# RWKV filler work on one Trainium2 core: one stream with a single share per unit, mixes between chains

## The chip, the cores and the metric

The kernel runs on one core of a Trainium2 chip. It is one program of four transformer layers in float32. The metric is the device time of one execution in microseconds. Before the change, three runs took 3275.48, 3282.33 and 3282.14 us, a median of 3282.14 us.

The core's engines are named as the profile names them: PE (matmul; PEld is its weight load), DVE (vector), ACT (scalar and activation functions), POOL (GpSimd) and SP (used here for its DMA queue). Each engine runs its own instructions in order and waits on semaphores for others. Some DMAs are issued from SP's queue and some from ACT's.

## The reference

There are 16 sequences of 100 tokens with 512 channels, and a context of 361 tokens for each. Layers 0 and 2 are cross attention (layer 2 with an MLP). Layers 1 and 3 are RWKV blocks, and only they are touched here. A block, cut to what matters (`_ln` is a layer norm with weights):

```python
xa = _ln(x, ln1_w, ln1_b)
sx = concat([state[:, 1:2] - xa[:, :1], xa[:, :-1] - xa[:, 1:]])       # difference of neighbouring tokens
xxx = tanh((xa + sx * maa_x) @ maa_w1).reshape(b, l, 5, 32)
xxx = einsum('blfd,fde->blfe', xxx, maa_w2)
xm = xa[:, :, None] + sx[:, :, None] * (maa_stack + xxx)               # five mixed inputs: k, w, v, r, g
xk, xw, xv, xr, xg = (xm[:, :, j] for j in range(5))
w = exp(-exp(time_decay + tanh(xw @ td_w1) @ td_w2))
r, k, v = xr @ Wr.T, xk @ Wk.T, xv @ Wv.T
g = silu(xg @ Wg.T)
# for each token, 32 heads of 16 channels, state s of 16 x 16 a head:
#   a = k_t v_t^T ; out_t = r_t (u * a + s) ; s = a + w_t * s
og = group_norm(out, gn_w, gn_b)
x1 = x + og * g @ Wo.T
xc = _ln(x1, ln2_w, ln2_b)                                             # channel mixing
sx2 = concat([state[:, 0:1] - xc[:, :1], xc[:, :-1] - xc[:, 1:]])
rr = sigmoid((xc + sx2 * ffn_maa_r) @ Wfr.T)
kk = square(relu((xc + sx2 * ffn_maa_k) @ Wfk.T))
x_out = x1 + rr * (kk @ Wfv.T)
```

## The kernel before

**Tiles.** The 16 sequences are four groups (`NG = 4`, `G = 4` sequences each), so a group's rows are `T = 400` tokens. Channels are four chunks of 128 (`NC = 4`). Activations lie as channels by tokens, 128 x 400, while a layer norm is computed on rows of tokens (100 x 512) and turned by PE transposes.

**The scan and its units.** The recurrence is computed by DVE scans along time. Chunk `C` of 16 (four per group) holds 128 channels of 400 tokens, and it is worked off in 8 units; a layer has `UNITS = 128`. One unit does two of the 16 value columns of each head. On PE, `spread` (two matmuls with `sel` into `vb`) spreads v over the head's rows, one unit ahead. Then come ACT's small copy of the start state into `vb`, DVE's `product` (`vb<-vb,kc`, v times k), two DVE scans (`a<-wc,vb`), POOL's `a<-a,rc` (times r) and, every second unit, PE's `gather` of two units into `acc`. A finished chunk passes through `norm` (the group norm: copies on ACT, the matmul with `mean`, Ln and Exp on ACT, products on POOL). `enter`, `bonus` and `gates` load a chunk's k, w, r, v and g from DRAM scratch on SP's queue and add the `u` term.

**The filler.** Everything else in the layer is cut into `pieces`, each with an estimated PE time in us, a first unit (`slot`) in which it may run, a function and a tag. Each turn of the loop over `u` emits the unit's own work and then takes pieces from the front of the list, skipping those whose slot has not come, until a share `due` of estimated time is used up. Pieces of time 0 are taken as soon as their slot comes. A chain (four matmuls that add up in one PSUM bank) is two pieces that follow each other directly. Instructions are pinned to this order on each engine, while DMAs are placed by a scheduler.

- `projections(g, base)` makes group g's k, v, r, w and g from x. First come the layer norm's `stats` (DVE), `root` (POOL) and `normed` (ACT). Then come `turned` (16 transposes in four pieces), `inner` (the chain with `w1`), `mix` (32-row matmuls with `maa_w2`, then DVE and POOL build the mixed input `xj`), `decay_in` and `decay`, `plain` (the chains with `Wk`, `Wv`, `Wr`) and the gates' chains with `Wg`. The `Wg` chains are kept in `held` and placed in the next group's list. Results are stored to DRAM scratch on ACT's queue; the scratch pool holds two groups.
- `channels(g, slot)` is the channel mixing. It has stats, `normed`, `turned`, keys (chains with `Wfk`), then `gates_of` (`Wfr`) and `values` (`Wfv`) for rows 0 to 3 by turns; rows 3 are a small product.
- `output(g, slot)` is the product with `Wo` and the residual, tag `("wo", g)`, placed at the front of the list when group g's units are done. Later work needs some of these done, and `through(tag)` forces them.

**The order around the change.** Projections of group 0 come before unit 0. Those of group g + 1 are appended at the unit 10 before group g ends (u = 22, 54 and so on). The channel mixing of groups 0 to 2 is appended in one go at u = 118 - 32 = 86, with the stats and transposes of a group placed inside the list of the group before it; that of group 3 at u = 128. In a group's list all mixes of a pair stand together, as do the decays. The share is 2.6 for the first 23 units, then 2.85, 3.7 in the last 32 units and 3.9 after them. Odd units and units 2 and 7 of a chunk get less, since they have work of their own.

Single-buffered tiles (`ext`, `sx`, `z0`, `tz`) and the rings `xm` (4), `tm` (4) and `stage` (6) limit how far groups may overlap, and three PSUM banks `mm` serve all pieces.

Of the kernel before, what the change touches and what calls it, by code (L numbers as in the profile page):

```python
# [17 lines left out]
NC = E // 128  # L18
G = 4
NG = B // G  # L20
# [16 lines left out]
def xattn_sequence(ctx: ExitStack, tc: tile.TileContext, d: dict, out: bass.AP):  # L37
# [196 lines left out]
    some = scratch.enter_context(tc.tile_pool(name="scratch", bufs=1))  # L234
# [462 lines left out]
    def rwkv(n, ws, small, first, next_weights, last):  # L697
# [6 lines left out]
        with ExitStack() as es:  # L704
# [3 lines left out]
                tc.tile_pool(name=f"l{n}a_dram", bufs=2, space=bass.MemoryType.DRAM)  # L708
# [26 lines left out]
            put = {}  # L735
# [133 lines left out]
            def projections(g, base):  # L869
# [59 lines left out]
                behind = [(p[0], base - 1 if g > 1 or i > 3 else -1000, *p[2:]) for i, p in enumerate(held)]  # L929
# [134 lines left out]
                for i in range(G):  # L1064
                    piece(0.0, lambda i=i: normed(i), base)
                for c in range(NC):
                    piece(0.45, lambda c=c: turned(c), base + 1)
                late = base + 2

                def mix(fs, c):  # L1070
                    piece(1.0 if len(fs) > 1 else 0.9, lambda: mixed(fs, c), late)

                pieces.extend(behind[:2])
                inner()
                pieces.extend(behind[2:6])
# [12 lines left out]
                for c in range(NC):  # L1088
                    plain(3, "Wr", "r", c)
                for c in range(NC):  # L1090
                    mix((4,), c)
                held[:] = written(lambda: [gate(co) for co in range(NC)])

            def channels(g, slot):


# [64 lines left out]
                def values(i):  # L1161
# [22 lines left out]
                some = lambda fn, n: written(lambda: [piece(0.01, lambda i=i: fn(i), slot) for i in range(n)])  # L1184
                root, normed = ln_apply(st, [xb[g * G + i] for i in range(G)], xn, nm)
                return {
                    "stats": some(stats, G) + written(lambda: piece(0.01, root, slot)),
                    "normed": some(normed, G),
                    "turned": written(lambda: [piece(0.45, lambda c=c: turned(c), slot) for c in range(NC)]),
                    "first": written(lambda: [keys(co) for co in range(NC)] + [gates_of(0), values(0)]),  # L1190
                    "second": written(lambda: [gates_of(1), values(1), gates_of(2), values(2)]),
                    "third": written(lambda: gates_of(3)),
                    "fourth": written(lambda: values(3)),
                }

            def channel_stream(groups, slot):

                got = []
                parts = [channels(g, slot) for g in groups]
                for k in ("stats", "normed", "turned"):  # L1200
                    got += parts[0][k]
                got += [(p[0], slot - 1, *p[2:]) for p in held]
                held.clear()
                for p, q in zip(parts, parts[1:] + [{"stats": [], "normed": [], "turned": []}]):
                    got += p["first"] + q["stats"] + p["second"] + q["normed"]
                    got += p["third"] + q["turned"] + p["fourth"]
                return got


# [138 lines left out]
            UNITS = 32 * NG  # L1348
            u, due = -42, 0.0
            while u < UNITS + 6 or pieces or slots.due or slots.late:  # L1350
# [3 lines left out]
                g = (u + 10) // 32  # L1354
                if u % 32 == 22 and g + 1 < NG:
                    projections(g + 1, u + 7)
                elif u % 32 == 22 and g + 1 == NG:
                    pieces.extend(channel_stream(range(NG - 1), u + 7))
                elif u % 32 == 0 and u > 0:
                    if u == UNITS:  # L1360

                        kept = max(len(pieces) - 4, 0)
                        for i in range(kept, len(pieces)):
                            pieces[i] = (pieces[i][0], u + 8, *pieces[i][2:])
                        own = channel_stream([NG - 1], u + 8)
                        pieces[kept:kept] = own[: G + 1]
                        pieces.extend(own[G + 1 :])
# [30 lines left out]
                due = min(due, 0.0) + (2.6 if 0 <= u < 23 else 2.85 if u < UNITS - 32 else 3.7 if u < UNITS else 3.9)  # L1398
# [369 lines left out]
    def load(layer, *names):  # L1768
        return {k: load_w(d[f"L{layer}_{k}"], f"l{layer}_{k}") for k in names}
# [80 lines left out]
```

## Time and profile before

One execution was profiled. Its own time is 3275.75 us; the span that the trace covers is 3274.0 us. Layers 1 and 3 have the same plan. The stretches below are cut at the first and last DVE product `vb<-vb,kc` of each layer; idle is the length less PE's busy time, and PEclk is the mean granted clock of PE as a share of full speed.

| stretch (us from the span's start) | length | PE busy | PE idle | DVE busy | POOL busy | PEclk |
|---|---|---|---|---|---|---|
| layer 1 before unit 0 (663.9 to 765.7) | 101.8 | 85.1 | 16.7 | 30.4 | 37.0 | 0.81 |
| layer 1, starts of units 0 to 127 (765.7 to 1356.6) | 590.9 | 527.6 | 63.3 | 444.9 | 400.3 | 0.89 |
| layer 1 after that (1356.6 to 1454.3) | 97.7 | 74.2 | 23.5 | 22.8 | 18.9 | 0.87 |
| layer 3 before unit 0 (2499.0 to 2598.9) | 99.9 | 85.1 | 14.8 | 28.9 | 33.5 | 0.80 |
| layer 3, starts of units 0 to 127 (2598.9 to 3182.7) | 583.8 | 521.3 | 62.5 | 444.8 | 400.2 | 0.90 |
| layer 3 after that (3182.7 to 3274.0) | 91.3 | 74.2 | 17.1 | 18.9 | 16.7 | 0.90 |

Mean durations of the instructions that recur, from the page's groups and the timeline: DVE product 982 ns, scan 973 ns (two a unit), the DVE part of a mix (`tm`) 624 ns, POOL's `a` product 1885 ns, the POOL part of a mix (`xj`) 961 ns. A PE matmul in float32 shows as two records of the same shape, while `spread` shows as one.

How to read it: an engine's busy time does not say that it sets the pace. PE is the busiest, but a busy PE may be running at half clock, and what ends its idle stretches is another engine's work. The stretches of a few units tell more than the whole loop, since the filler is not the same from one to the next.

### The profile page before, as it was taken

The numbers are of one execution on the slowest core, as the hardware profiler recorded it, in microseconds if no ns is written. First come the engines' busy times: TensorE is split into PE (matmuls) and PEld (weight loads), VectorE is DVE, ScalarE is ACT, GpSimd is POOL, SyncE is SP. The second block draws the span as 40 slices with busy tenths as digits, with TensorE's granted clock in tenths as the row PEclk, the third lists the DMA queues.
The fourth block names the chain that finished last, engine by engine and source line by source line (L and its number), as shares of the span: only waits on it lengthen the run. The fifth ranks groups of instructions, "written<-read, shape, count | busy, mean of one in ns | idle before, by whom it ended". The sixth has DMA issues, their size and how long they took to land. (4 is left out here: it accounts for less than half of the span.)

```text
span 3274.0 us, 44343 instructions
## 1 busy us (share of the span) xinstructions
PE 2970.2 (91%) x16403; PEld 1523.1 (47%) x16403; DVE 1647.3 (50%) x3309; ACT 1235.9 (38%) x2883; POOL 1161.1 (35%) x1058
## 2 busy tenths in 40 slices
PE   7999898888898989879999999899998998898997
PEld 4555555534344444334555555445554443444443
DVE  2555555625877777523433333321001388877761
ACT  4777677722423343322232323211111233334332
POOL 0111111135677675422212111210001467676651
PEclk9999999978889899989999999999998888999998
DMA  6101010022222432130000010020011322324211
GB/s 195 33 23 33 23 41 18 1 88 71 91 84 89 131 102 86 47 101 20 20 21 20 21 33 19 27 70 11 7 52 30 108 96 69 104 83 135 89 32 51
DMA packets 134690, 193.98 MB, mean 59 GB/s; under 512 B 19806, under 2 KB 102686, under 8 KB 134474
## 3 DMA queue, kind: packets, MB, share of 16 engines
q1 hardware_dynamic: 102218, 145.26, 14.8%
q10 hardware_dynamic: 32256, 45.89, 3.8%
q8 instruction: 129, 2.11, 0.3%
q14 instruction: 87, 0.71, 0.1%
HBM read 115.20 MB, written 49.15 MB: 50 GB/s over the span
## 5 line engine op out<-in xcount | busy, mean ns | idle before, releaser
L88 POOL TENSOR_TENSOR a<-a,rc 128x800 f32<-128x800 f32 x256 | 481.6, 1885 | 245.7 <-DVE a L88 194.5
L88 DVE TENSOR_TENSOR_SCAN a<-wc,vb 128x400 f32<-128x400 f32 x512 | 477.3, 973 | 42.3 <-PE acc L93 20.8
L88 DVE CUSTOM_DVE_ANT_0 pr<-l_sc,mask 100x361 f32<-100x361 f32 x512 | 252.0, 528 | 144.8 <-PE l_sc L93 144.7
L88 DVE TENSOR_TENSOR vb<-vb,kc 128x792 f32<-128x792 f32 x256 | 251.5, 982 | 136.6 <-ACT vb L88 135.4
L88 ACT ACTIVATE pr<-pr,nm 100x361 f32<-100x361 f32 x512 | 301.3, 593 | 4.6 <-POOL sums L88 3.7
L96 PEld LDWEIGHTS l_pT<-ident,pr 100*121 100x121 f32 x1536 | 193.2, 186 | 103.8 <-issue 50.4
L93 PE MATMUL vb<-xc,sel 128*128 128x400 f32 x512 | 217.9, 509 | 12.4 <-DVE a L88 12.2
L1542 DVE CUSTOM_DVE_ANT_0 junk<-l2a_sc,mask 100x361 f32<-100x361 f32 x256 | 136.9, 535 | 182.3 <-PE l2a_sc L93 165.1
L96 PE MATMUL l_pT<-ident,pr 100*121 100x100 f32 x1536 | 216.3, 276 | 6.3 <-ACT pt L88 4.3
L1578 POOL TENSOR_TENSOR pa<-pt,pt 121x1600 f32<-121x1600 f32 x16 | 57.1, 3571 | 364.1 <-ACT pt L1573 364.1
L88 ACT COPY vb<-s 128x8 f32<-128x8 f32 x256 | 44.3, 173 | 365.4 <-PE vb L93 329.8
L88 ACT COPY pt<-l_pT 121x400 f32<-121x400 f32 x256 | 125.1, 489 | 146.5 <-PE l_pT L96 145.6
L88 POOL TENSOR_TENSOR xj<-tm,ext 128x400 f32<-128x400 f32 x160 | 149.5, 961 | 82.9 <-DVE tm L88 82.9
L93 PE MATMUL v<-l_v_w,ct 128*121 128x512 f32 x384 | 177.2, 605 | 0.0
L1763 DVE TENSOR_TENSOR x<-pb,x 100x512 f32<-100x512 f32 x16 | 12.9, 804 | 320.0 <-DMA pb<-po 311.1
L74 PE MATMUL h<-yTb,l_fc 128*128 128x400 f32 x512 | 172.8, 500 | 0.6 <-ACT yTb L339 0.6
L93 PE MATMUL k<-ct,l_k_w 128*128 128x361 f32 x512 | 170.7, 476 | 0.0
L74 PE MATMUL p<-l_proj,h 128*128 128x512 f32 x384 | 165.5, 592 | 0.0
L93 PEld LDWEIGHTS vb<-xc,sel 128*128 128x128 f32 x512 | 99.5, 208 | 131.8 <-issue 80.9
L88 POOL TENSOR_SCALAR ve<-mv 100x1 f32<-100x1 f32 x16 | 3.6, 223 | 406.8 <-DVE mv L88 406.8
L88 DVE SCALAR_TENSOR_TENSOR tm<-mm,vec,sx 128x400 f32<-128x400 f32 x160 | 94.6, 624 | 102.5 <-PE mm L93 90.9
L93 PE MATMUL l_sc<-kz,qz 32*100 32x361 f32 x1024 | 112.2, 508 | 34.3 <-DVE nm L88 32.1
(282 smaller groups left out, 5194.2 us busy)
## 6 DMA issues: line engine op xcount, KB each, us to landing
ct<-in_ctxT SPq DMA_DIRECT2D x32, 722.0 KB
dk<-k ACTq DMA_DIRECT2D x32, 200.0 KB
kc<-dk SPq DMA_DIRECT2D x32, 200.0 KB
dw<-wd ACTq DMA_DIRECT2D x32, 200.0 KB
wc<-dw SPq DMA_DIRECT2D x32, 200.0 KB
dv<-v ACTq DMA_DIRECT2D x32, 200.0 KB
dhi<-hi ACTq DMA_DIRECT2D x32, 200.0 KB
dlo<-lo ACTq DMA_DIRECT2D x32, 200.0 KB
```

The lines of the kernel that those rows point to most:

```text
L74: nc.tensor.matmul(out=ps, lhsT=lhs(c), rhs=rhs(c), start=(c == 0), stop=(c == n - 1))
L88: return lambda *args, **kw: tc.keep_in_program_order(op(*args, **kw))
L93: pin(nc.tensor.matmul(**kw))
L96: pin(nc.tensor.transpose(out, in_, ident))
L1542: nc.vector.tensor_tensor_reduce(out=junk, in0=ss[r][:L, :S2], in1=t["mask"], scale=-1.0, scalar=FLT_MAX, op0=ALU.add, op1=ALU.min, accum_ ...
L1578: nc.gpsimd.tensor_tensor(t["pa"], t["pt"][0], pt, ALU.add)
L1763: nc.vector.tensor_tensor(x, pb[:, i, :], x, ALU.add)
```

## The change

The change is in the function `rwkv` alone. The diff, cut to its core:

```diff
-                tc.tile_pool(name=f"l{n}a_dram", bufs=2, space=bass.MemoryType.DRAM)
+                tc.tile_pool(name=f"l{n}a_dram", bufs=3, space=bass.MemoryType.DRAM)
...
-                behind = [(p[0], base - 1 if g > 1 or i > 3 else -1000, *p[2:]) for i, p in enumerate(held)]
+                behind = list(held)
...
-                    piece(0.0, lambda i=i: normed(i), base)
+                    piece(0.0, lambda i=i: normed(i), base - 1 + i // 2)
                 for c in range(NC):
-                    piece(0.45, lambda c=c: turned(c), base + 1)
-                late = base + 2
+                    piece(0.45, lambda c=c: turned(c), base + 1 + c if g else base + 1)
+                late = base + (5 if g else 2)
...
-                pieces.extend(behind[:2])
+                pieces.extend(behind[:4])
                 inner()
-                pieces.extend(behind[2:6])
                 for c in range(NC):
                     mix((0, 1), c)
+                    pieces.extend(behind[4 + 2 * c : 6 + 2 * c])
                 decay_in()
-                pieces.extend(behind[6:])
                 for c in range(NC):
                     plain(0, "Wk", "k", c)
-                for c in range(NC):
                     mix((2, 3), c)
-                for co in range(NC):
-                    piece(0.9, lambda co=co: decay(co), late)
                 for c in range(NC):
                     plain(2, "Wv", "v", c)
+                    piece(0.9, lambda c=c: decay(c), late)
                 for c in range(NC):
                     plain(3, "Wr", "r", c)
-                for c in range(NC):
                     mix((4,), c)
...
-            def channels(g, slot):
+            def channels(g, base, pace):
+                slot = base + (3 if pace else 1)
...
+                    "stats": written(
+                        lambda: [piece(0.0, lambda i=i: stats(i), base - 6 + i) for i in range(G)]
+                        + [piece(0.0, root, base - 2)]
+                        + [piece(0.0, lambda i=i: normed(i), base - 1 + i // 2) for i in range(G)]
+                    ),
+                    "turned": written(lambda: [
+                        piece(0.45, lambda c=c: turned(c), base + 1 + (c // 2 if pace else 0)) for c in range(NC)
+                    ]),
+                    "rest": written(
+                        lambda: [keys(co) for co in range(NC)]
+                        + [fn(i) for i in range(4) for fn in (gates_of, values)]
+                    ),
...
-            def channel_stream(groups, slot):
...
+            def channel_stream(g, slot, pace=True):
+                part = channels(g, slot, pace)
+                pieces.extend(part["stats"])
+                pieces.extend(held)
                 held.clear()
...
+                pieces.extend(part["turned"] + part["rest"])
...
-            UNITS = 32 * NG
-            u, due = -42, 0.0
+            UNITS, LEAD = 32 * NG, (24.0, 30.0)
+            u, due, blended = -42, 0.0, 0
...
-                if u % 32 == 22 and g + 1 < NG:
-                    projections(g + 1, u + 7)
-                elif u % 32 == 22 and g + 1 == NG:
-                    pieces.extend(channel_stream(range(NG - 1), u + 7))
...
-                    output(g - 1, u + 7)
-                if u == UNITS - 32 - 3:
-                    cm.update(load(n, "Wfk", "Wfr", "Wfv"))
+                if u == UNITS:
+                    for i in range(max(len(pieces) - 8, 0), len(pieces)):
+                        pieces[i] = (pieces[i][0], u + 9, *pieces[i][2:])
+                if u % 32 == 0 and 0 < u <= UNITS:
+                    output(u // 32 - 1, u + 7)
+                short = sum(p[0] for p in pieces) < LEAD[len(put) == NG]
+                if u == -42:
+                    projections(0, u + 7)
+                elif short and u > -16 and len(put) < NG:
+                    projections(len(put), u + 8)
+                elif short and len(put) == NG and blended < NG:
+                    g = blended
+                    if u >= 32 * g + 40 and not any(p[3] == ("wo", g) for p in pieces):
+                        if g == 0:
+                            cm.update(load(n, "Wfk", "Wfr", "Wfv"))
+                        channel_stream(g, u + (8, 8, 4, 2)[g], g < NG - 1)
+                        blended += 1
...
-                due = min(due, 0.0) + (2.6 if 0 <= u < 23 else 2.85 if u < UNITS - 32 else 3.7 if u < UNITS else 3.9)
+                due = min(due, 0.0) + (2.9 if 0 <= u < UNITS else 3.9)
```

In words: projections and channel mixing are appended when the estimated time of the pieces left falls below 24 us (30 us once all projections are in the list), in the order of the groups, instead of at fixed units. The share is 2.9 in every unit of the loop. Mixes and decays stand between chains one at a time. The stats, the normalised rows and the transposes of a group get slots a unit or half a unit apart. The channel mixing of groups 1 to 3 is no longer woven into the one before. The weights of the channel mixing are asked for when its first group is appended, and the DRAM scratch holds three groups.

More of the change, by code (lines that the diff above doesn't have):

```diff
@@ L1182, in values @@
                     )
-                some = lambda fn, n: written(lambda: [piece(0.01, lambda i=i: fn(i), slot) for i in range(n)])
                 root, normed = ln_apply(st, [xb[g * G + i] for i in range(G)], xn, nm)
                 return {
[L1187 to L1193, printed above, removed]
-                }
@@ L1196, in channel_stream @@
-            def channel_stream(groups, slot):
[L1198 to L1202, printed above, removed]
+                    "stats": written(
[3 more added lines that the diff above has]
+                    ),
@@ L1203, in channel_stream @@
                 held.clear()
[L1204 to L1207, printed above, removed]
+                pieces.extend(part["turned"] + part["rest"])
             chunks = {}
@@ L1353, in rwkv @@
                     nws[""] = first_stats(f"a{n}", vector, gpsimd)
-                g = (u + 10) // 32
-                if u % 32 == 22 and g + 1 < NG:
-                    projections(g + 1, u + 7)
-                elif u % 32 == 22 and g + 1 == NG:
-                    pieces.extend(channel_stream(range(NG - 1), u + 7))
[L1359 to L1367, printed above, removed]
-                    output(g - 1, u + 7)
-                if u == UNITS - 32 - 3:
-                    cm.update(load(n, "Wfk", "Wfr", "Wfv"))
+                if u == UNITS:
[15 more added lines that the diff above has]
+                        blended += 1
                 if u >= UNITS and set(nws) <= {""} and not any(p[3] == ("wo", NG - 1) for p in pieces):
```

## The prediction, made before the changed kernel ran

> **What bounds the kernel now.** I read first the page's totals and slices, then where the span lies: the two RWKV stages fill 664 to 1454 us and 2499 to 3274 us.
>
> ```profile
> span 3274.0 us, 44343 instructions
> PE 2970.2 (91%) x16403; PEld 1523.1 (47%) x16403; DVE 1647.3 (50%) x3309; ACT 1235.9 (38%) x2883; POOL 1161.1 (35%) x1058
> PE   7999898888898989879999999899998998898997
> PEclk9999999978889899989999999999998888999998
> ```
>
> PE is busy 91% of the span, and its clock falls below nine tenths only inside the two RWKV stages (slices 8 to 17 and 30 to 39). Second, I cut layer 1's stage into windows. A unit starts at a DVE product `vb<-vb,kc`; the timeline has unit 0 at 765.7 us and unit 127 at 1356.6, so the main loop takes 590.9 us (583.8 in layer 3, from 2598.9). Rows are 8 units each: units 16, 24, 48, 80, 88 and 96 onwards, then the stretch after unit 127 begins.
>
> ```profile
> core 0: us, PE busy (x) PEld busy (x) DVE busy (x) ACT busy (x) POOL busy (x), PEclk, DMA share, GB/s
> 663.90:765.70 101.80, 85.10 (x236) 42.84 (x236) 30.37 (x47) 30.66 (x55) 37.00 (x55) 0.81 0.32 102
> ...
> 840.30:870.60 30.30, 25.12 (x105) 12.35 (x104) 27.11 (x36) 10.04 (x22) 21.41 (x17) 0.94 0.34 111
> 870.60:903.10 32.50, 25.27 (x97) 12.00 (x96) 25.24 (x32) 13.19 (x27) 23.36 (x21) 0.71 0.18 57
> ...
> 978.40:1010.30 31.90, 29.84 (x123) 14.08 (x122) 26.56 (x33) 15.24 (x32) 20.15 (x25) 0.99 0.44 152
> ...
> 1121.40:1152.00 30.60, 28.76 (x113) 13.64 (x112) 25.13 (x30) 15.32 (x33) 19.54 (x24) 0.98 0.67 221
> 1152.00:1192.20 40.20, 30.37 (x122) 15.34 (x122) 28.93 (x40) 14.70 (x29) 27.02 (x25) 0.87 0.33 102
> 1192.20:1232.10 39.90, 38.49 (x143) 18.20 (x142) 28.48 (x37) 17.22 (x36) 27.23 (x23) 1.00 0.25 76
> ...
> 1356.60:1377.80 21.20, 17.04 (x53) 6.65 (x51) 9.82 (x15) 6.51 (x9) 5.83 (x8) 1.00 0.29 87
> ```
>
> Units 16 to 31 give PE too little (25 us of work in 30 to 32), units 96 onwards too much (38.5 in 39.9), and rows with neither still differ: 3.8 to 4.0 us a unit where chains run alone at clock 0.98 to 0.99, 5.0 us at 0.87 where layer norm and transposes fall together. Over the sixteen rows PE is busy 527.6 us, DVE 444.9; PE is idle 63.3 us, and length times (1 - PEclk) adds up to 65 us.
>
> Third, the clock. These windows hold a burst of maa mixes and decays, and a run of chains.
>
> ```profile
> 811.00:825.00 14.00, 14.00 (x42) 5.11 (x34) 8.96 (x12) 6.49 (x13) 10.49 (x14) 0.50 0.15 58
> 842.00:862.00 20.00, 20.00 (x87) 10.33 (x86) 17.36 (x20) 9.13 (x19) 11.12 (x9) 1.00 0.32 111
> ```
>
> PE has no gap in either, yet the first runs at half speed. In the timeline its matmuls are mixes over 32 rows and decays over 64; the second's are chains over 128. [...]
>
> Last, PE's timeline where it stops:
>
> ```profile
> 806.45 2.88 PE L93 MATMUL mm<-z,maa_w2a 32*128 32x400 f32 x8 [1.36 <-DVE rk L88]
> 1184.76 0.43 PE L96 MATMUL mm<-ident,xn_1b 100*128 100x100 f32 x1 [7.49 <-ACT xn_1b L88]
> 1270.39 3.54 PE L93 MATMUL mm<-xk_1b,l_Wfk 128*128 128x400 f32 x4 [5.00 <-POOL xk_1b L88]
> 1377.76 4.54 PE L93 MATMUL mm<-l_Wo,gc 128*128 128x512 f32 x6 [4.16 <-POOL gc L88]
> ```
>
> Bursts, each time: four mixes in a unit wait for DVE and POOL, transposes for a layer norm issued in one go, keys for POOL's mixes, the last output for the group norm.
>
> **The change, part by part.** No matmul or vector operation is added or removed; what moves is read from the order in which the two built programs issue PE's instructions, cut at the spreads.
>
> *Even share.* Of units 0 to 125, 29 hold no matmul of a chain before and 4 after (7, 24, 25, 56). The 29 take 150 us by the starts of their products, 5.2 each. Sixteen transposes between two spreads stood in four units and now in one (116); the others come four or eight at a time. Four or more mixes stood in 8 units, now in one (24, with six). The channel mixing's `bn_stats` go one to a unit; before, four of them (0.68 + 0.18 us each) stand in a row on DVE ahead of a product at 1226 us. I price the main loop anew from the two rows of chains at full clock: (31.90 + 30.60)/16 = 3.91 us a unit, 128 units = 500 us. On top:
> - DVE. The two rows hold 25.8 us of it, the mean row 27.8; 2.0 x 16 = 32 us more, partly beside PE. Bounds 0 and 32; PE is the busier there (94% against 83%), so half: +16.
> - Keys still follow the transposes directly, three times in the loop (units 84, 98, 116), now without the small `Wfv` that stood between. The row at 1270 gives 5.00, and 1.03 stood ahead of its transposes: 6.0 each, +18 (bounds 0, and 28 if each costs a 7.49 and a 2).
> - Three projections begin with transposes, `w1` chain, mixes in dependence. Units 31 and 33 took 6.35 and 6.20, 4.7 above two units of 3.91; I take 4 each, +12 (0 to 14).
> - Slow clock left over: 65 us of loss before, 11 of it in the starved rows and 35 in the rows with mix bursts. Chains now stand between the mixes, so I leave +12 (0 to 40).
>
> Sum 558 us, against 590.9 and 583.8: -33 and -26.
>
> [...]
>
> *Tail.* After unit 126's spread 4 `Wfr` and 6 `Wfv` matmuls over 512 columns fewer remain: 10 x 0.925 us (eight records took 3.70) = 9.3. They run in the loop now, inside its 3.91 a unit, where the units given up by the first items leave room; in the tail they were the cover of the group norm. The bare chain from the last product at 1356.6, by the timeline's durations: scans to 1359.5, POOL `a` to 1361.6, gather 0.9, two ACT copies 1.0, `mean` 1.0, two tables with Ln and Exp 3.7, POOL 1.02, ACT 0.72, POOL 1.03 = 1371, against 1377.8. I take -6 a layer (bounds 0 and -9.3). The pieces held for later stay the same four, so the rest of the tail is unmoved.
>
> *Before unit 0.* One `w1` chain and four mixes of group 1 move ahead of the first spread: 8 matmuls at 0.71 (eight records of a `Wr` chain took 2.85) = +5.7. Group 0's later mixes and its decays now alternate with chains, in a stretch that loses 101.8 x 0.19 = 19 us to the clock; I take 5 back. Net 0 (bounds -10 and +6).
>
> *Moved transfers.* Projections run up to a group ahead, hence the third DRAM buffer; that costs no engine anything. The loads of `Wfk`, `Wfr`, `Wfv` move forward on SP among the loads for chunks 9 to 11. Each waits for the last use of `Wk`, `Wv`, `Wr` (units 62, 68, 78), and queued behind them are loads of those chunks, needed from units 72, 80 and 88; the weights come free first, so 0. Without that cover a chunk load would be late by its wait and the product of that unit with it. The four small loads of `ox` that SP now issues first read rows done in layer 0: 0. Stores stay on ACT's queue; the store of `lo` waits there for DVE as before.
>
> Total: -33 - 26 - 12 + 0 = -71. The profiled execution took 3275.75 us (span 3274.0), so 3204.7; the median of the runs shown is 6.4 higher, so **3211 us**.
>
> **The rivals.**
> *Clean loop:* no stall and no slow clock left beyond the two terms for transposes: 500 + 18 + 12 = 530 a loop, -61 - 54 - 12 = -127, 3155 us. For it: rows at 3.83. Against: they hold no mix at all, which costs DVE 0.62 and POOL 0.96 each.
> *Only starvation goes:* DVE (3.48 us busy a unit, little under PE) becomes the bound and orders stalls as before; only the starved rows' 12.4 us of idle falls to the 2 of others, -8 a loop, with the tails -28: 3254 us.
> [...]
>
> **How the numbers follow.** Forecast 0.58 (its own range 3170 to 3245), clean loop 0.14, only starvation 0.13, slow clock 0.15. About 0.2%, 6.6 us, is what measurement can tell from no change. Faster: 0.58 + 0.14 + 0.10 = 0.82; the same 0.03, out of the third case; slower 0.15. The lowest sum (all lower bounds) is below the clean loop's 3155; I end the range there, less 5 us for its own scatter; above, 3268 includes the third case and leaves out the slow clock.
>
> **What would show it.** Sixteen rows of 8 units each between 30 and 39 us, none of 40; PEclk above 0.93 in the loop; idle PE in it near 40 us; no row with PE under 27 us busy; 15 us instead of 21 from unit 127's product to the last part of `Wo`. I am wrong if PEclk in units 24 to 46 stays near 0.6, if DVE's idle does not shrink though PE's load is even, or if SP's queue holds chunk loads behind the weights.

## The result and the profile after

The changed kernel takes **3307.06 us** (median of 4 runs, 3298.99 to 3309.4), the kernel before 3280.46 us beside it. The ratio is 1.0079 with a 95% interval of 1.0058 to 1.010: 0.8% slower. The forecast was 3211 us, with a range up to 3268.

The page of the changed kernel begins like this (totals, then PE's busy tenths and clock in 40 slices):

```profile
span 3307.6 us, 44349 instructions
PE 2965.7 (90%) x16403; PEld 1503.0 (45%) x16403; DVE 1650.3 (50%) x3309; ACT 1236.4 (37%) x2883; POOL 1162.4 (35%) x1058
PE   7999898888899888879999999899998898888887
PEclk9999999987898899979999999999998798988998
```

PE is busy 4.5 us less than before, with as many instructions, in a span 33.6 us longer. So the extra time is time in which PE waits, and the totals don't say where. Cuts by stage do: at the first layer-norm transpose of a layer, at the product of unit 0, at the product of unit 127. (The first cut lies 6.8 us later than in the table ahead of the prediction, so that stretch of layer 1 is 95.0 us here and 101.8 there.)

| stretch, us | before | after | difference | predicted |
|---|---|---|---|---|
| layer 1, first transpose to unit 0 | 95.0 | 116.0 | +21.0 | 0 |
| layer 1, units 0 to 127 | 590.9 | 588.3 | -2.6 | -33 |
| layer 1, from unit 127 to the next stage | 97.8 | 93.8 | -4.0 | -6 |
| layer 3, first transpose to unit 0 | 94.4 | 115.8 | +21.4 | 0 |
| layer 3, units 0 to 127 | 583.8 | 586.6 | +2.8 | -26 |
| layer 3, from unit 127 to the end | 91.3 | 83.0 | -8.3 | -6 |
| all else (layers 0 and 2) | 1720.8 | 1724.1 | +3.3 | 0 |

Two things went wrong: 21 us a layer ahead of unit 0, and a loop that gained nothing. Windows of layer 1 in the changed kernel follow (length, then busy time of the engines, PEclk, DMA share, GB/s): the stretch ahead of unit 0, then units 16-23, 24-31, 56-63 and 80-87, and the 15 us from unit 127's product to the last part of `Wo`.

```profile
674.10:790.10 116.00, 97.73 (x262) 45.62 (x264) 31.61 (x50) 31.24 (x56) 43.75 (x60) 0.78 0.29 88
855.80:888.30 32.50, 29.50 (x128) 14.69 (x128) 25.95 (x31) 16.96 (x34) 26.50 (x25) 1.00 0.24 75
888.30:934.50 46.20, 39.89 (x132) 16.11 (x132) 30.65 (x41) 9.50 (x21) 32.15 (x27) 0.78 0.15 44
1045.50:1086.20 40.70, 33.75 (x130) 13.96 (x130) 29.43 (x39) 9.69 (x21) 27.55 (x22) 0.86 0.30 93
1160.00:1202.80 42.80, 34.56 (x137) 17.16 (x140) 25.00 (x31) 18.20 (x38) 29.72 (x25) 0.84 0.38 119
1378.40:1393.40 15.00, 10.40 (x31) 3.77 (x31) 5.92 (x12) 5.92 (x8) 5.64 (x7) 0.89 0.29 88
```

Read the second line against the third. By count PE has the same to do in both, 128 and 132 matmuls; the first does it in 32.5 us at full clock, the second needs 46.2 at 0.78, with PE "busy" for 39.9 of them. The last line is the 15 us that the prediction named for the tail.

Ahead of unit 0, PE's timeline in the changed kernel (start, duration, operation, in brackets the idle time before it and who ended it):

```profile
754.68 2.51 PE L93 MATMUL mm<-xj,l_Wg 128*128 128x400 f32 x7
762.98 0.43 PE L96 MATMUL mm<-ident,xn_a 100*128 100x100 f32 x1 [5.79 <-ACT xn_a L88]
...
769.01 1.70 PE L93 MATMUL mm<-xm,maa_w 128*128 128x400 f32 x2 [1.48 <-POOL xm L88]
771.52 1.70 PE L93 MATMUL mm<-xm,maa_w 128*128 128x400 f32 x2 [0.81 <-POOL xm L88]
...
778.84 4.20 PE L93 MATMUL mm<-z,maa_w2a 32*128 32x400 f32 x8 [0.59 <-ACT z L88]
782.97 1.03 PE L93 MATMUL vb<-xc,sel 128*128 128x400 f32 x2
783.80 1.53 PE L93 MATMUL mm<-rk,ones 128*128 128x400 f32 x2
785.27 4.19 PE L93 MATMUL mm<-z,maa_w2a 32*128 32x400 f32 x8
```

And DVE's at the same place, where the first product `vb<-vb,kc` stands:

```profile
780.65 1.96 DVE L88 SCALAR_TENSOR_TENSOR tm<-mm,vec,sx 128x400 f32<-128x400 f32 x3 [20.64 <-PE mm L93]
783.14 0.64 DVE L88 SCALAR_TENSOR_TENSOR tm<-mm,vec,sx 128x400 f32<-128x400 f32 x1 [0.53 <-PE mm L93]
785.37 0.57 DVE L88 TENSOR_TENSOR rk<-mm,vc 128x400 f32<-128x400 f32 x1 [1.59 <-PE mm L93]
787.07 1.18 DVE L88 SCALAR_TENSOR_TENSOR tm<-mm,vec,sx 128x400 f32<-128x400 f32 x2 [1.12 <-PE mm L93]
789.56 0.64 DVE L88 SCALAR_TENSOR_TENSOR tm<-mm,vec,sx 128x400 f32<-128x400 f32 x1 [1.32 <-PE mm L93]
790.11 0.98 DVE L88 TENSOR_TENSOR vb<-vb,kc 128x792 f32<-128x792 f32 x1
```

The same place in the kernel before, PE and then DVE:

```profile
745.50 11.58 PE L93 MATMUL mm<-xj,l_Wg 128*128 128x400 f32 x32
...
762.82 1.02 PE L93 MATMUL vb<-xc,sel 128*128 128x400 f32 x2
...
765.70 0.98 DVE L88 TENSOR_TENSOR vb<-vb,kc 128x792 f32<-128x792 f32 x1
```

In the changed kernel the last `Wg` matmul of group 0 ends at 757.2. What follows on PE belongs to group 1: layer norm, transposes, the `in` chain (the one with `w1`) with a wait for POOL before each of its quarters, mixes at 0.52 us a record. Only then come the spread of unit 0 (782.97) and, behind further reads of group 1's mixes on DVE, its product. From the end of `Wg` to the first product it takes 32.9 us, against 8.6 before (757.1 to 765.7). DVE stands idle for 20.64 us of it, and so do the scans. As windows, first before, then changed, then the run e1 below, which starts group 1 later (from the end of its `Wg`, 752.2):

```profile
757.10:765.70 8.60, 5.27 (x20) 3.07 (x20) 1.06 (x2) 7.39 (x14) 3.97 (x6) 0.72 0.31 92
757.20:790.10 32.90, 21.77 (x46) 9.45 (x48) 6.85 (x13) 9.55 (x16) 15.61 (x20) 0.56 0.12 31
752.20:764.10 11.90, 3.10 (x11) 1.82 (x10) 2.12 (x5) 5.90 (x10) 3.84 (x8) 0.63 0.24 69
```

Of the 24.3 us that the change adds here, PE is busy for 16.5 and idle for 7.8, and its clock is 0.56. Of the 21.0 us that e1 takes away again, 18.7 are busy time. The part up to group 0's last `Wg` matmul is 3.3 us shorter than before (83.1 us against 86.4).

### The profile page after: what moved, and what is told of

It is laid out like the page before. It is cut to its first block, busy times and chain, and to the rows that moved or that the text cites. A ratio compares the mean times of both kernels' runs of the same rounds, so it can differ in the third digit from the quotient of the medians.

```text
span 3307.6 us, 44349 instructions
## 1 busy us (share of the span) xinstructions
PE 2965.7 (90%) x16403; PEld 1503.0 (45%) x16403; DVE 1650.3 (50%) x3309; ACT 1236.4 (37%) x2883; POOL 1162.4 (35%) x1058
## 5 line engine op out<-in xcount | busy, mean ns | idle before, releaser
L1757 DVE TENSOR_TENSOR x<-pb,x 100x512 f32<-100x512 f32 x16 | 13.2, 825 | 321.2 <-DMA pb<-po 312.0
L93 PE MATMUL l_sc<-kz,qz 32*100 32x361 f32 x1024 | 113.3, 512 | 34.4 <-DVE nm L88 32.1
```

The source lines that it names most:

```text
L93: pin(nc.tensor.matmul(**kw))
L1757: nc.vector.tensor_tensor(x, pb[:, i, :], x, ALU.add)
```

## The experiments

Each ran beside the kernel before on the same chip; ratios are to that kernel, with the 95% interval. "Ahead" is the stretch from the first transpose to unit 0, "loop" units 0 to 127. These and the last column come from one profiled execution each, which can lie some 10 us from the median (3234.0 us in e1, 3253.8 in e3, 3279.5 in e4, 3293.9 in e12), so a few us between two loops are not to be built on.

| run | median us | ratio [interval] | ahead L1 / L3 | loop L1 / L3 | unit 127 to the end, L3 |
|---|---|---|---|---|---|
| before (profile) | 3280.46 | 1 | 95.0 / 94.4 | 590.9 / 583.8 | 91.3 |
| changed | 3307.06 | 1.0079 [1.0058, 1.010] | 116.0 / 115.8 | 588.3 / 586.6 | 83.0 |
| e1 group 1 later | 3244.49 | 0.9894 [0.9878, 0.991] | 95.4 / 95.0 | 574.1 / 570.2 | 84.9 |
| e2 old order | 3311.35 | 1.0104 [1.009, 1.0118] | 118.9 / 118.7 | 586.2 / 585.5 | 85.8 |
| e3 before + order alone | 3263.57 | 0.9953 [0.994, 0.9966] | 92.0 / 94.4 | 577.3 / 577.0 | 91.4 |
| e4 append sooner | 3288.77 | 1.0046 [1.0031, 1.006] | 116.1 / 116.1 | 577.9 / 577.0 | 82.2 |
| e5 = e1 + e4 | 3244.51 | 0.9907 [0.9892, 0.9921] | 94.7 / 94.5 | 572.3 / 574.0 | 84.9 |
| e6 = e1 + transposes sooner | 3257.13 | 0.994 [0.9928, 0.9953] | 95.1 / 94.4 | 581.6 / 579.8 | 87.9 |
| e7 before + share alone | 3285.09 | 1.0037 [1.0023, 1.0051] | 103.5 / 102.8 | 560.3 / 560.1 | 112.5 |
| e8 = e1 + e4 + e6 | 3263.35 | 0.9962 [0.9949, 0.9974] | 95.0 / 94.4 | 585.4 / 582.8 | 86.4 |
| e10 = e1 + `rk` later | 3235.55 | 0.988 [0.9863, 0.9897] | 98.0 / 94.6 | 567.1 / 565.7 | 89.9 |
| e11 = e6 + `rk` later | 3209.83 | 0.9794 [0.9778, 0.981] | 95.2 / 94.9 | 553.1 / 555.8 | 86.7 |
| e12 changed + `rk` later | 3285.98 | 1.003 [1.002, 1.0041] | 115.1 / 114.3 | 577.5 / 573.8 | 84.8 |

### e1: group 1 appended three positions later

```diff
-                elif short and u > -16 and len(put) < NG:
+                elif short and u > -13 and len(put) < NG:
```

> The changed kernel with group 1's projections appended three positions later (from u > -13 instead of u > -16), so that its `in` chain and all its mixes come behind the spread of unit 0 instead of ahead of it; everything else as changed. Theory (the 21 us a layer ahead of unit 0 are the chain of layer norm, transposes, `in` and first mixes of group 1, which stand ahead of the first product on TensorE and on VectorE): the stretch from the first layer-norm transpose to the product of unit 0 falls from 116 us to 93-100 in both layers, the loop grows by 0 to 9 us a layer because it now holds that work under the scan, and the whole is 3262-3288 us, 0.994 to 1.003 of the kernel before. Rival 1 (the 21 us are work that only changed place): the stretch falls and the loop grows by as much, the whole stays at 3298-3312. Rival 2 (the alternation inside group 0 costs them): the stretch stays at 112-118.

With this one number, PE issues eight of group 1's sixteen transposes ahead of the spread of unit 0, and the `in` chain and all mixes after the spread of unit 2. The windows are: ahead of unit 0, the loop, and the row of units 24-31.

```profile
668.70:764.10 95.40, 79.12 (x226) 37.99 (x226) 26.98 (x42) 27.52 (x50) 31.99 (x48) 0.84 0.32 104
764.10:1338.20 574.10, 505.47 (x2126) 234.27 (x2127) 445.75 (x550) 217.20 (x447) 401.97 (x352) 0.93 0.28 89
867.50:909.60 42.10, 34.64 (x139) 15.78 (x138) 28.82 (x37) 13.62 (x28) 30.87 (x27) 0.88 0.14 47
```

The stretch is back at 95 us in both layers, and the loop, which now holds that work, is not longer but 14 to 16 us shorter. The first rival falls (the loop did not grow by what the stretch lost), and the second (the stretch did not stay). Part of the price did come back: units 0 to 18 take 5.7 us more in layer 1 and 7.0 in layer 3, of the 20.6 and 20.8 taken away. The whole, 3244, is below the theory's 3262 to 3288: I had not expected the loop to shrink. In layer 1 it gains 8.0 us in units 19 to 34, 3.2 in units 48 to 60 and 6.7 in units 61 to 82. Groups 2 and 3 start three to five units later than in the changed kernel; that this is the reason was not tested by itself. PE's busy time in the loop fell by 12.9 us (518.4 to 505.5) with the clock up from 0.91 to 0.93, its idle time by 1.3. The row of units 24-31 is still 42 us, since group 2 starts in it.

### e2 and e3: the order, taken out of the changed kernel and put alone into the one before

e2 puts the old list back into `projections` of the changed kernel:

```diff
...
                 for c in range(NC):
                     plain(0, "Wk", "k", c)
+                for c in range(NC):
                     mix((2, 3), c)
+                for co in range(NC):
+                    piece(0.9, lambda co=co: decay(co), late)
                 for c in range(NC):
                     plain(2, "Wv", "v", c)
-                    piece(0.9, lambda c=c: decay(c), late)
...
```

The parts left out put the held `Wg` chains back in three lots and the mixes for the gates (4) back in a row.

e3 is the whole of that diff the other way round, on the kernel before.

> The changed kernel with the old order inside a group's projections (mixes of one kind together, decays together, gate chains in three lots); the stream, the share of 2.9, the leads and the group 1 start stay as changed. Theory A (alternating is a gain, the loss comes from elsewhere): bare mixes and decays bring stalls and the half clock, the loop grows by 5 to 20 us a layer and the stretch ahead of unit 0 by about 3, the whole is 3318-3350 us. Theory B (alternating takes the three banks in turn faster than VectorE and GpSimd read them, and that is why the loop gained nothing): the loop shrinks by 10 to 30 us a layer and the whole is 3250-3290 us.

> The kernel before with only the alternating order inside a group's projections; its appending at fixed units, its shares of 2.6, 2.85 and 3.7 and its channel stream stay. Theory A (alternating is a gain by itself): group 0's own part ahead of unit 0 is 3 us shorter (95 to about 92), the loop 0 to 12 us a layer shorter, the whole 3250-3276 us, 0.991 to 0.999 of the kernel before. Theory B (alternating costs, through the banks): the loop is longer by 5 to 25 us a layer, the whole 3285-3330 us.

Alternating is a gain by itself: 0.5% in the kernel before, as theory A had it. There the loops are 13.6 and 6.8 us shorter, the 3 us ahead of unit 0 show in layer 1 alone, PE's busy time in layer 1's loop fell from 527.5 to 511.0 us, and the clock's loss (length times one minus PEclk) from 66 to 45. Taking it out of the changed kernel (e2) cost 2.9 us a layer ahead of unit 0, as theory A had it, but nothing in the loop, where more slow clock (68 against 50 us of loss) and less idle time (57 against 70) cancel; the 3311 us of the whole are under theory A's 3318 to 3350. The intervals of e2 and the changed kernel overlap. Theory B, that the alternation is what hurts, falls in both runs: without it the loops are 2.1 and 1.1 us shorter, not 10 to 30.

### e4 and e5: groups 2 and 3 appended sooner

```diff
-            UNITS, LEAD = 32 * NG, (24.0, 30.0)
+            UNITS, LEAD = 32 * NG, (28.0, 30.0)
```

> The changed kernel with a lead of 28 us instead of 24 for the projections: groups 2 and 3 are appended while more pieces are left, so that the held gate chains are not used up while their transposes wait for their slots, and the first mixes have gate chains between them. Theory (bare mixes at units 24 to 26 and the half clock that they bring are the largest part of what the loop lost): the row of units 24-31 falls from 46 us to 34-38, the rows of 48-63 by 0 to 6 together, the whole falls by 16 to 30 us to 3277-3292. Rival (the rows are long because of waits on GpSimd and VectorE that any order has, the clock follows): the row stays above 42 and the whole within 8 us of 3307.

> The changed kernel with group 1's start three positions later (as in the run of that kind, 3244 us) and the lead of 28 us as well (alone it took the changed kernel from 3307 to 3289 us). If the two losses are separate, the gains add: row of units 24-31 from 42 to 34-37 us, the whole 3220-3232 us. Rival (the later start of group 1 already moves group 2 on, so that gate chains are left between its mixes): the row stays at 38-43 and the whole at 3236-3248.

The rows of units 16-23 and 24-31 in e4:

```profile
849.70:887.30 37.60, 32.64 (x138) 15.61 (x138) 27.25 (x34) 15.82 (x32) 31.09 (x26) 0.95 0.22 69
887.30:921.90 34.60, 30.94 (x127) 13.60 (x123) 29.26 (x39) 9.50 (x21) 25.73 (x22) 0.95 0.18 57
```

The second needs 34.6 us in place of 46.2, PE is busy 30.9 in place of 39.9, and the clock is 0.95 in place of 0.78. But group 2 now starts earlier, and the first row took over part of it, 37.6 us in place of 32.5: the two together gain 6.5 us, not 11.6. In the changed kernel the held `Wg` chains had been used up in units 17 to 22, while group 2's transposes waited for their slots, and its first mixes stood alone; with 4 us more lead four `Wg` half chains stand between them. The loops are 10 us shorter, 6.5 of them in units 19 to 34, where group 2 starts, and 2.7 in units 48 to 60, where group 3 does (layer 1). In units 19 to 34 the clock's loss fell from 11.9 to 5.1 us and PE's idle time only from 9.3 to 8.6, so slow clock was what went. Whether the cover did it is not shown by itself, since PE's wait for `rk` at this start also fell, from 5.40 to 1.32 us. Nor is the loss separate from e1's: there group 2 starts some three units later and has chains left between its mixes, and e5 gains nothing on e1. The rival was right for e5 (rows of 38.0 and 39.2 us).

### e7: the equal share alone, in the kernel before

```diff
-                due = min(due, 0.0) + (2.6 if 0 <= u < 23 else 2.85 if u < UNITS - 32 else 3.7 if u < UNITS else 3.9)
+                due = min(due, 0.0) + (2.9 if 0 <= u < UNITS else 3.9)
```

> The kernel before with only the equal share of 2.9 us a unit in place of 2.6, 2.85 and 3.7; order, appending at fixed units and channel stream stay. Theory (the share alone moves work from the last 32 units into the tail and starves units 22-31 sooner): the four last rows fall from 164 us to 140-155 a layer, the tail from the last product on grows by 8 to 25, rows 16-31 stay or grow, the whole 3265-3292 us. Rival (the equal share is what the change gains by itself): the whole falls to 3235-3262.

Its windows of layer 1: ahead of unit 0, and the loop.

```profile
668.80:772.30 103.50, 91.29 (x250) 46.18 (x250) 28.01 (x45) 31.27 (x56) 37.63 (x54) 0.79 0.30 98
772.30:1332.60 560.30, 504.53 (x1985) 234.20 (x1986) 441.81 (x545) 199.93 (x418) 382.94 (x331) 0.88 0.29 89
```

A loop of 560 us looks like the prediction come true. It isn't a gain: the loop holds 1985 matmul records where the loop of the kernel before holds 2120; 14 of the rest stand ahead of unit 0, the others behind unit 127 (the end of layer 3 grew from 91.3 to 112.5 us, the four last rows of the loop in layer 1 fell from 164 to 136, below the 140 to 155 I had expected). The whole is 3285, as the theory had it. A shorter stage has to be read with the number of instructions in it. The other new thing is the 103.5 us ahead of unit 0, which I had not expected: the new expression also raises the share of the positions before unit 0, from 2.85 to 3.9, and so more mixes of group 1 stand ahead of unit 0's product. On DVE it shows:

```profile
771.73 0.63 DVE L88 SCALAR_TENSOR_TENSOR tm<-mm,vec,sx 128x400 f32<-128x400 f32 x1 [8.12 <-PE mm L93]
772.28 0.98 DVE L88 TENSOR_TENSOR vb<-vb,kc 128x792 f32<-128x792 f32 x1
```

One read of a mix, which waits 8.12 us for PE's `in` chain and mix, and the product behind it: 8.5 us more ahead of unit 0, by one instruction's place.

### e6, e10, e11, e12: where GpSimd is late

In e1 PE's largest waits in layer 1's loop are these (us in total, times, longest):

```profile
PE mm L93 <- POOL rk L88: 14.0, 8, 3.1
PE mm L93 <- POOL xk_1b L88: 12.4, 3, 5.0
```

The second is the channel mixing: its transposes stand directly ahead of the `Wfk` chain that needs what POOL makes of them. e6 puts them ahead of work that is still in the list:

```diff
 def channel_stream(g, slot, pace=True):
...
-                pieces.extend(part["stats"])
+                at = max(len(pieces) - 6, 0) if g else len(pieces)
+                pieces[at:at] = part["stats"] + part["turned"]
                 pieces.extend(held)
                 held.clear()
-                pieces.extend(part["turned"] + part["rest"])
+                pieces.extend(part["rest"])
```

The first is the `ones` matmul of each chunk, which reads `rk`, a POOL product issued one unit before. e10 (on e1), e11 (on e6) and e12 (on the changed kernel) put that matmul one unit later, and with it the smaller share of the unit that holds it:

```diff
-                    elif at == 7:
-                        bonus(C, 1)
                 C = u // 8
+                if 0 <= C < NC * NG and at == 0:
+                    bonus(C, 1)
...
-                due -= 0.45 * (u % 2) + 0.7 * (at in (2, 7)) if unit else 0.0
+                due -= 0.45 * (u % 2) + 0.7 * (at in (0, 2)) if unit else 0.0
```

> The changed kernel with group 1's start three positions later, and in the channel mixing the transposes put ahead of work that is still there (ahead of the held gate chains for group 0, ahead of the last six half chains for groups 1 and 2) instead of directly in front of the `Wfk` chain that needs them. In the run without this, TensorE stands 5.05, 3.82 + 4.00 and 3.32 us at these three places of layer 1, about 16 us a layer. Theory (these waits for GpSimd's and ScalarE's mix are a third loss of the loop): the gaps fall below 1 us each, the loop by 6 to 16 us a layer, the whole to 3212-3232 us. Rival (VectorE and GpSimd have as much to do and the scans come no sooner): the gaps go but the whole stays within 6 us of 3244.

> The changed kernel with group 1's start three positions later (3244 us) and the `ones` matmul of each chunk one unit later: it reads `rk`, which GpSimd makes, and TensorE waited 14.0 us for it in layer 1's loop, 8 times. Theory (these waits are real and the next instruction isn't waiting as long): that wait falls to 0-4 us, the loop by 4 to 11 us a layer, the whole to 3222-3237 us. Rival (GpSimd is late as a whole, and the scans' or the mixes' wait takes its place): within 6 us of 3244.

> As the run with the channel mixing's transposes sooner (3257 us; TensorE's wait for `rk` grew there from 14.0 to 34.6 us in layer 1's loop), and the `ones` matmul one unit later. If `rk` alone ate the gain of the sooner transposes, that wait falls below 10 us, the loop by 12 to 25 us a layer and the whole to 3205-3228 us, under the run with the later matmul alone. If GpSimd's burst of subtractions and mixes is itself too long for one unit, waits for other GpSimd tiles take the place, and the whole stays at 3235-3258 us.

> The changed kernel with nothing but the `ones` matmul of each chunk one unit later. TensorE waited 18.8 us for `rk` in layer 1's loop. Theory (lateness of GpSimd's `rk` is part of why the loop gained nothing): that wait falls to 0-6 us, the loop by 6 to 16 us a layer, the stretch ahead of unit 0 stays at 110-117, the whole 3275-3296 us. Rival: within 6 us of 3307.

e6 made it slower than e1, outside both expectations. Its waits of PE, and PE's and POOL's timelines at unit 88:

```profile
PE mm L93 <- POOL rk L88: 34.6, 9, 9.1
```

```profile
1154.22 0.84 PE L93 MATMUL vb<-xc,sel 128*128 128x400 f32 x2
1163.34 1.70 PE L93 MATMUL mm<-rk,ones 128*128 128x400 f32 x2 [8.28 <-POOL rk L88]
```

```profile
1152.31 1.68 POOL L88 TENSOR_TENSOR sx_1b<-ext_1b 128x400 f32<-128x400 f32 x2
1153.93 0.98 POOL L88 TENSOR_TENSOR xk_1b<-mxk_1b,ext_1b 128x400 f32<-128x400 f32 x1
...
1157.61 1.88 POOL L88 TENSOR_TENSOR a<-a,rc 128x800 f32<-128x800 f32 x1
1159.43 1.04 POOL L88 TENSOR_TENSOR gc<-gc,og 128x400 f32<-128x400 f32 x1
1160.42 1.88 POOL L88 TENSOR_TENSOR a<-a,rc 128x800 f32<-128x800 f32 x1
1162.25 1.04 POOL L88 TENSOR_TENSOR rk<-rc,rk 128x400 f32<-128x400 f32 x1
```

POOL has no gap from 1147.7 to 1163.3. The transposes hand it four subtractions and eight mixes at once, `rk` waits its turn behind them, and PE, which could do `Wg` chains meanwhile, stands in its own order at the `ones` matmul. The wait for `xk` went and one for `rk` took its place, with the clock at 0.54 over the 6.7 us after it.

If that is the cause, both edits together must give what neither gives alone. They do. Beside e1's 0.9894, the sooner transposes alone make 0.994, the later matmul alone 0.988 (not to be told from e1: the intervals overlap), both together **0.9794**, 3209.83 us, as the theory had it. PE's wait for `rk` falls from 34.6 to 3.8 us, and the loops are 28.5 and 24.0 us shorter than e6's, rather more than the 12 to 25 expected. (e10 by itself did what its theory said, with `rk` down to 1.7 us and loops 7.0 and 4.5 us shorter, but the stretches around the loop took part of that back, 98.0 us ahead of unit 0 and 89.9 at the end.) e11's loop and two rows that were long before, units 80-87 and 88-95:

```profile
768.40:1321.50 553.10, 499.10 (x2120) 231.31 (x2121) 447.12 (x549) 214.50 (x447) 401.19 (x352) 0.96 0.30 93
1118.60:1153.80 35.20, 30.38 (x128) 15.32 (x130) 25.97 (x32) 19.11 (x38) 29.03 (x27) 0.98 0.37 119
1153.80:1189.60 35.80, 35.80 (x128) 17.41 (x129) 28.91 (x37) 12.20 (x27) 23.54 (x15) 0.92 0.32 90
```

The loop has 2120 matmul records, as the changed kernel's has 2122, and takes 35 us less (31 in layer 3). e12 shows the same in the changed kernel itself: nothing but the `ones` matmul a unit later, and PE's wait for POOL's `rk`, 18.8 us there, no longer appears. Waits for other POOL tiles took part of its place (`xk` from 13.2 to 18.8 us, `xm` from 0.4 to 6.8); the loop falls by 10.8 and 12.8 us, and the stretch ahead of unit 0 stays at 115. The whole is 3286, within what the theory gave.

### e8: all three of e1, e4 and e6

The edits are those shown above.

> The changed kernel with all three: group 1's start three positions later, the lead of 28 us, the channel mixing's transposes ahead of remaining work. If the three losses are separate and add: loops of 550-562 us a layer, as the prediction had them, and a whole of 3200-3222 us. If the waits only move to the next engine: loops of 565-575 and 3230-3245 us.

Loops of 585 and 583 us: neither expectation. It behaves like e6 (the intervals overlap): the lead gains nothing once group 1 starts later, and the wait for `rk` that the sooner transposes bring is in it as well, 35.2 us in layer 1's loop.

## Why the prediction was wrong, step by step

**Before unit 0: predicted net 0, measured +21 a layer. This step failed.** I priced what moved there as PE work, eight matmuls at 0.71 us, and took 5 us back for group 0's own part. That part did get 3.3 us shorter. But from group 0's last `Wg` matmul to unit 0's product it takes 24.3 us more and not 5.7: PE is busy for 16.5 of them and idle for 7.8. The price of 0.71 is that of a chain at full clock, and here the clock was 0.56; I counted up to the spread, while eight more records of mixes and DVE's reads of them stand between it and the product; and there was no wait in the price. The larger part is thus PE's own work at about half its clock, standing in order ahead of unit 0; the waits are the smaller. The work is a chain over four engines: ACT normalises, PE transposes, POOL mixes, PE runs `in`, ACT does the tanh, PE the mixes, DVE reads them. Ahead of unit 0 there is no scan yet, and PE's spread and DVE's product of unit 0 stand in order behind it. e1 takes the `in` chain and the mixes away from there, and 20.6 and 20.8 us with them; in the loop they cost 5.7 and 7.0. My upper bound of +6 came from the busy time of one engine. I also overlooked that the share ahead of unit 0 rises from 2.85 to 3.9. In the kernel before, this by itself costs 8.5 us in layer 1 and 8.4 in layer 3 (e7); in e1, which keeps that share, the stretch is back at 95 us all the same, so it is not a loss to be added to the other.

**The loop: predicted -33 and -26, measured -2.6 and +2.8.** The 3.91 us a unit was not wrong: units 16-23 of the changed kernel take 4.06. But the stretch holds 127 units from start to start and I multiplied by 128, 3.9 us too much. The terms on top were what failed. This is the time above 3.91 a unit in layer 1, in us, by where it falls (units by starts of products, unit 126 the last):

| units | before | changed | e11 |
|---|---|---|---|
| 0-18 | 11.3 | 4.3 | 9.2 |
| 19-34 (group 2 starts) | 6.5 | 19.7 | 7.0 |
| 35-47 | 7.2 | 2.8 | 4.4 |
| 48-60 (group 3 starts in the changed kernel and e11) | 0.0 | 12.9 | 8.2 |
| 61-82 | 17.6 | 17.6 | 8.1 |
| 83-103 (channel mixing of group 0; of group 1 too in the changed kernel and e11) | 17.2 | 16.6 | 11.0 |
| 104-126 | 34.5 | 17.8 | 8.5 |
| sum | 94.3 | 91.7 | 56.5 |

- *Even share:* right in the main. The overfull last rows give 17 us back and units 35-47 another 4. The 7 us of the first units are not the share's: with the same share and group 1 back in the loop, they lose 10.0 us in e1 and 9.2 in e11, so that gain was work that stood ahead of unit 0.
- *Three projections begin, 4 us each, +12:* by place, this is the term that was most mis-sized. Where groups 2 and 3 start, the changed kernel loses 32.6 us, against 4 each in the forecast; at units 30 to 34 the kernel before lost 8.4 (its third start lies in the row of 61-82). Two things meet there in the changed kernel: group 2's first mixes have no chain between them, and a wait of 5.40 us for `rk` at 885.9 falls on this start, with a clock of 0.55 after it. e4 and e12 each lose less (13.2 and 10.2, 14.4 and 8.2 us), but in both the first mixes have chains between them and the wait for `rk` is short (1.32 and 1.0 us), while in e12 one of 5.6 us for `xm` stands at the same start. How much each cause costs stays open.
- *Slow clock left over, +12:* by kind, this one was off the most. The 12 was an estimate that no run shows; the loss was 50 us, against 66 before. The two overlap, since 18.7 of the 50 lie where groups 2 and 3 start; 25.5 lie in units 61 to 126. e3 shows that the alternation lowers the loss, to 45 in the kernel before, but chains between the mixes never brought it near 12 (24.8 in e11).
- *Keys directly after the transposes, 6 each, +18:* the waits themselves were priced about right, 13.2 us for `xk` in layer 1's loop against three of 5.00. The excess of units 83 to 126, 34.4 us, was larger, though not all of it is keys. Here, as at the starts, I had asked what PE does and not whether POOL can: 12 POOL instructions come due at once, and its `rk` for the next chunk is queued behind them. I never priced `rk`; PE's wait for it rose from 8.6 to 18.8 us in layer 1's loop.
- *DVE, +16:* not tested by itself.

**Tail: predicted -6, measured -4.0 and -8.3.** Right, with the 15 us to the last part of `Wo`. **Moved transfers: 0.** No wait for a weight or chunk load is among PE's larger waits of the loop, and DVE's waits for DMAs in layer 1's loop are 17.7 us against 15.1 before, 0.7 of them for a chunk load.

**The rivals.** In mechanism "only starvation goes", 3254 us, comes nearest: the starved rows did go and the loop gained little. The slow clock, to which I gave the 0.15 of a slower kernel, is the only rival on the right side of no change, but the clock's loss in layer 1's loop went down, from 66 to 50 us. What made the kernel slower, a start of unit 0 held up by the next group, was none of my rivals. Of the signs I had named for being right, two failed clearly: there are rows of 46.2, 42.8, 40.9 and 40.7 us, and PE is idle for 70 us in place of 40. Of those for being wrong, the clock in units 24 to 46 did not stay near 0.6 (0.78, then 0.95 twice), but DVE's idle time hardly shrank, from 146.0 to 142.5 us.

In e11, with the start put right and POOL's lateness taken off PE, the excess is 56.5 and 59.2 us where I had 58, and the kernel takes 3210 us. That this is near the 3211 of the forecast shows what the plan could give with the start put right and these waits gone; that the sums agree is in part luck. It doesn't make the steps right, since e11 holds three edits that the change didn't, and its loop still loses 24.8 us to the clock, where I had left 12. What stays open: how what e1 gains on the changed kernel in the loop divides between clock and waits, since moving group 1's start moves those of groups 2 and 3 too. The 6.9 us for which PE waits in unit 77 of e1 and of e11 (for the read of `ox` on DVE) were not tried.

## What to carry to other kernels

Price work that moves across the start of a pipelined loop as a chain over all its engines, with its waits and at the clock it will have, not as busy time of one engine at full clock: work estimated at 5.7 us took 24 us ahead of unit 0, and 6 to 7 us inside the loop (e1). Where pieces alternate on one engine, count what each hands to the next engine at once and what is queued there behind it; in e6 the wait for `xk` that was taken away came back at a later instruction of that queue (`rk`, from 14.0 to 34.6 us), and two edits that are each worth nothing or less can together be worth 1% (e6 and e10 against e11). And compare a stage's time only together with the number of instructions in it (e7), and a row's only together with its neighbours, since work can move from one to the next (e4).

## What the hardware showed that was not expected

In the changed kernel PE's clock was low directly after a wait (0.55), and again a little later while PE was busy throughout (0.50). After the 5.40 us that PE waited for `rk` from 885.9 us on, these windows of the changed kernel follow; the first is the stretch ahead of that wait, and the third overlaps the end of the second:

```profile
878.00:885.90 7.90, 7.52 (x32) 3.94 (x24) 5.22 (x7) 3.32 (x8) 7.16 (x7) 1.00 0.24 73
891.40:898.00 6.60, 6.46 (x16) 2.38 (x16) 2.33 (x3) 0.47 (x2) 3.06 (x2) 0.55 0.14 35
897.40:900.70 3.30, 3.02 (x12) 1.38 (x11) 1.64 (x4) 0.60 (x2) 2.06 (x3) 1.00 0.24 62
900.80:911.00 10.20, 10.20 (x32) 3.18 (x34) 8.55 (x12) 1.25 (x4) 7.96 (x8) 0.50 0.00 0
```

The clock is 1.00 before and 0.55 directly after the wait. It comes back to 1.00 for some 3 us and then falls to 0.50 for 10 us, although PE has no gap there (10.20 of 10.20 busy): besides two spreads, those are mixes over 32 rows, gathers into 32 columns and matmuls over 64 columns. The low clock after a wait was there in layer 1's loop of the kernel before as well: behind PE's three longest waits (3.78, 7.49 and 5.00 us, which end at 869.9, 1184.8 and 1270.4), the windows of 869.9 to 873.0, 1184.8 to 1187.8 and 1270.4 to 1273.4 read 0.50 each. So in the changed kernel the clock went down twice here, once after a wait and once while PE ran a burst of small matmuls, as in the full row at 811 us of the kernel before (14.00 of 14.00 us busy, clock 0.50). No run here tests by itself whether the small shapes are the reason, and the clock was not low in every such burst. In e4 the same kinds of matmul ran for 7.3 us at full clock:

```profile
893.10:900.40 7.30, 6.63 (x40) 2.15 (x39) 6.71 (x11) 1.18 (x4) 6.28 (x7) 1.00 0.07 28
```
